# Two gates of a recurrent cell as four 64 by 64 products on the quarters of the TensorE array

## The chip, the core and the metric

The kernel runs on one NeuronCore of a Trainium2 chip. The metric is device time of one execution in microseconds. The granted TensorE clock was 0.999 of full speed in the profiled execution.

## The reference, cut to what matters

A stack of graph layers works on 3327 nodes with 64 features and a dense adjacency matrix `adj` (3327 by 3327). The first layer is two gated cells, one after the other, each with its own weights:

```python
def _ggc(x, adj, W, wih, whh, bih, bhh):
    m = adj @ (x @ W)
    gi = m @ wih.T + bih
    gh = x @ whh.T + bhh
    i_r, i_z, i_n = jnp.split(gi, 3, axis=-1)
    h_r, h_z, h_n = jnp.split(gh, 3, axis=-1)
    r = jax.nn.sigmoid(i_r + h_r)
    z = jax.nn.sigmoid(i_z + h_z)
    n = jnp.tanh(i_n + r * h_n)
    return (1.0 - z) * n + z * x
```

Three more layers follow: a ranked neighbour sum whose weights come from the order of the nonzeros in a row of `adj`, three products with the element-wise square of `adj`, and two plain hops with tanh. A layer norm with ReLU stands before each layer.

The change concerns the line of `n` in the second cell. There `h_n` and `i_n` must be kept apart, since `r` multiplies only the one; for `r` and `z` the two parts are simply added.

## The kernel before

**Layout.** The nodes are padded to 26 blocks of 128 and form two halves of 13 blocks. The halves are stacked on the 128 partitions, 64 features each. The destination nodes are cut into chunks of blocks (`CH`): chunks 0, 1 and 2 are 384 columns wide, chunk 3 is 512. Chunks 0 and 1 form one group, 2 and 3 the other. For each of the eight products with the matrix (numbered k = 0 to 7) and each chunk, L607 adds up two products per source block, one for each half, into the two partition halves of a PSUM bank. Only one group's matrix tiles are loaded at a time (`slots`, 20 buffers), and two consecutive products share the tiles where they can (`joint`).

**Order.** Each engine's order is written out by the program itself: `run` walks a list of units, and `propagate` issues a unit's matmuls. What follows a finished sum is a Python generator (`after_1` for the second cell), which is advanced between units as its counted-down time runs out (`spend`). So the instructions of a cell lie between the matmuls of the next sums, and between the mask builds of L466 on VectorE, which make 0/1 masks for the ranked product k = 2.

**Banks.** There are eight PSUM banks, four named `sum` and four named `temp`. `take` hands out the one that was given back longest ago; `give` returns it. The products of the gates, the mask products with `tri` (L307, followed by L521 on VectorE or L523 on ScalarE) and the transposes all draw on them.

**The cell.** `gru` first moves the finished sum into `both[c]` (L824 on ScalarE for one half of the nodes, L825 on VectorE for the other). `both[c][:, s]` has 128 rows for half `s`: the neighbour sum `m` in rows `upper(s)` and the state `x` in rows `upper(1 - s)`. `cells[:, cell, s, g, :]` holds the matching 128 by 64 weights of gate `g`: 0 and 1 are `r` and `z`, with weights in all 128 rows. Gate 2 is `h_n` and has weights in rows `upper(1 - s)` only, and gate 3 is `i_n`, in rows `upper(s)` only; the other rows are zero.

`gate(g)` (L873 to L877) takes one bank and issues two products of 128 rows by 64 columns, one per half of the nodes. The gates 0 and 1 go through a sigmoid on ScalarE (L881). Then L886 computes `(h_n + bias) * r` and L888 adds `i_n`, both on VectorE over all 128 partitions. L897 is the tanh on ScalarE, and L901 to L903 mix with `z` and the old state. In the first cell `h_n` was computed earlier by `ahead_of_cell`, so only the second cell runs gate 2 here. After the cell, `after_1` transposes the result back (L307), adds it to `xs` (L854) and runs the layer norm (L834 to L849) ahead of k = 2.

A matmul of f32 operands appears as two records in the profile, each with its weight load. All matmuls of this kernel are listed with 128 rows and 64 columns (128*64).

Of the kernel before, what the change touches and what calls it, by code (L numbers as in the profile page):

```python
# [13 lines left out]
ALU = mybir.AluOpType  # L14
# [77 lines left out]
def upper(n):  # L92
    return slice(n * D, (n + 1) * D)
# [3 lines left out]
def kernel(  # L97
# [9 lines left out]
    nc = tc.nc  # L107
# [16 lines left out]
    cells = const.tile([P, 2, 2, 4, D], F32, name="cells")  # L124
# [3 lines left out]
    both = [const.tile([P, 2, (b1 - b0) * P], F32, name=f"both{c}") for c, (b0, b1) in enumerate(CH[:NC])]  # L128
    both += [both[1][:, :, (CH[c][0] - CH[1][0]) * P:(CH[c][1] - CH[1][0]) * P] for c in PARTS]
    bcol = const.tile([P, NBIAS], F32, name="bcol")  # L130
# [57 lines left out]
    ahead = {}  # L188
# [110 lines left out]
    def width(c):  # L299
        return blocks(c) * P  # L300
# [15 lines left out]
    def take(sums=False, either=True):  # L316


        either = either and not sums
        pool = idle_sums if sums else idle_temps  # L320
        if either and idle_sums and (not pool or released[idle_sums[0]] < released[pool[0]]):
            pool = idle_sums
        for c in list(tasks):
            if not pool and c not in running:
                advance(c)
        i = pool.popleft()
        return i, banks[i]

    def give(i):
        released[i] = max(released) + 1  # L330
        (idle_sums if i < 4 else idle_temps).append(i)
# [21 lines left out]
    def advance(c):  # L353
        running.add(c)
        try:
            tasks[c][1] = next(tasks[c][0])
        except StopIteration:
            del tasks[c]
        running.discard(c)
# [463 lines left out]
    def evacuate_stacked(acc, c):  # L823
        nc.scalar.copy(both[c][upper(0), 0], acc[0][1][upper(0), :width(c)])  # L824
        nc.vector.tensor_copy(both[c][upper(1), 1], acc[1][1][upper(1), :width(c)])  # L825
        for i in {acc[0][0], acc[1][0]}:
            give(i)
# [37 lines left out]
    def gru(acc, c, bi, bh, cell, pace=1.0):  # L865

        w = width(c)
        evacuate_stacked(acc, c)
        yield 0.8 * pace
        at = dead.popleft()  # L870
        r, z, d = (slots[at].rearrange("p s w -> p (s w)")[:, i * CWM:i * CWM + w] for i in range(3))

        def gate(g):  # L873
            i, ps = take()
            for s in range(2):
                nc.tensor.matmul(ps[upper(1 - s), :w], cells[:, cell, s, g, :], both[c][:, s], start=True, stop=True)  # L876
            return i, ps  # L877

        for g, v in enumerate((r, z)):
            i, ps = gate(g)  # L880
            nc.scalar.activation(v, ps[:, :w], AF.Sigmoid, bias=bsum[:, cell, g:g + 1])  # L881
            give(i)
        nh = None if cell == 0 else gate(2)
        ni = gate(3)
        yield 1.0 * pace
        nc.vector.scalar_tensor_tensor(r, ahead[c] if nh is None else nh[1][:, :w], bcol[:, bh + 2:bh + 3], r,  # L886
                                       op0=ALU.add, op1=ALU.mult)
        nc.vector.tensor_tensor(r, r, ni[1][:, :w], ALU.add)  # L888
        give(ni[0])
        if nh is not None:  # L890
            give(nh[0])
        else:
            del ahead[c]
            if not any(ch in ahead for ch in GROUPS[c // 2]):
                rooms[c // 2].free()
        yield 1.0 * pace
        nc.scalar.activation(r, r, AF.Tanh, bias=bcol[:, bi + 2:bi + 3])  # L897
        yield 0.8 * pace
        for s in range(2):
            u = upper(1 - s)  # L900
            nc.vector.tensor_tensor(d[u], both[c][u, s], r[u], ALU.subtract)  # L901
        nc.vector.tensor_tensor(d, d, z, ALU.mult)
        nc.vector.tensor_tensor(d, d, r, ALU.add)  # L903
        if cell == 0:
            nc.vector.tensor_scalar(both[c][upper(0), 1], d[upper(0)], 0.0, None, op0=ALU.max)
        yield 2.4 * pace
        if cell == 0:
            nc.scalar.activation(both[c][upper(1), 0], d[upper(1)], AF.Relu)
            yield 1.0 * pace
        return at, d  # L910
# [27 lines left out]
    def after_0(c, acc):  # L938
        at, _ = yield from gru(acc, c, BI1, BH1, 0)
        dead.append(at)  # L940
        i, v = stacked_to_nodes(c, lambda s: ident[:, upper(1 - s)])
        yield 0.8
        yk = nodes(c)
        nc.vector.tensor_copy(flat(yk), v)
        give(i)
        y[1][c] = yk

    def after_1(c, acc):
        pace = 1.0 if c in GROUPS[0] else 1.2
        at, h2T = yield from gru(acc, c, BI2, BH2, 1, pace)  # L950
        v = transpose_to_nodes(h2T, c)
        dead.append(at)
        yield 0.8 * pace
        residual(v, c, relu=True)
        yk = nodes(c)
        yield from layernorm_relu(yk, c, TWO27, 1.2 * pace, squares_on_scalar=c in GROUPS[1])
        y[2][c] = yield from in_three(yk, c)
        yield 80.0 if c in GROUPS[1] else 14.0
        add_row(c, 3)
# [126 lines left out]
```

## Time and profile before

| | |
|---|---|
| time, median of 3 runs | 708.03 us (707.58 to 708.05) |
| the profiled execution's own time | 707.41 us |
| its span | 705.5 us |
| TensorE matmul busy | 680.6 us (96%), 5100 records |
| VectorE busy | 351.7 us (50%), 747 records |
| ScalarE busy | 271.3 us (38%), 421 records |
| GpSimd busy | 75.7 us (11%), 114 records |
| DMA | 201.31 MB, mean 285 GB/s |

The span runs from the first to the last instruction; the profiled execution's time is 1.9 us longer. Busy shares are means over stages that differ: the matrix streams through with little VectorE work in most of the span, while from some 180 to 330 us mask builds, ranked products and squares fill VectorE and ScalarE. The second cell runs at 163 to 231 us. Below, PE is TensorE, DVE is VectorE, ACT is ScalarE, POOL is GpSimd and SP is SyncE. In the chain of waits, a line has the start, the length and the engine, tile and line of one link; "issue" is time in which no wait is visible. In the timeline, a line has the start, the length, the engine, the line, the operation, out<-in, the shapes and the count, and in brackets the idle time before it with what ended it. In the table of stretches, the numbers are busy microseconds and instruction counts of each engine.

### The profile page before, as it was taken

What the parts mean: (1) busy time and instruction counts of PE and PEld (TensorE: products, weight loads), DVE (VectorE), ACT (ScalarE), POOL (GpSimd) and SP (SyncE); (2) the same over time, 40 slices, a digit from 0 to 9 for tenths busy, and PEclk for the clock granted to TensorE, in tenths of its full rate; (3) what the DMA queues carried; (4) which work ended last, traced back from release to release, by engine and by line L of the source; (5) the groups of instructions that cost most, each with busy time, mean ns of one, the idle gap of its engine ahead of it and who ended that gap; (6) DMA issues with size and microseconds to landing.
All of it is one profiled execution on the core that took longest, in us unless ns stands there. A gap on an engine that the chain in (4) does not pass through costs nothing.

```text
span 705.5 us, 12624 instructions
## 1 busy us (share of the span) xinstructions
PE 680.6 (96%) x5100; PEld 362.5 (51%) x5100; DVE 351.7 (50%) x747; ACT 271.3 (38%) x421; POOL 75.7 (11%) x114
## 2 busy tenths in 40 slices
PE   1999999999999999999999999999999999999997
PEld 1454666643545787677444444333344444344464
DVE  7566835633997889847533105425271565005101
ACT  1014100212136888888997206832166500000101
POOL 4300000002291233111100000000000000000000
PEclk9999999999999999999999999999999999999999
DMA  9999996089688952683799649963997399917991
GB/s 337 401 387 404 405 406 239 1 337 384 204 284 299 313 176 83 241 296 103 266 369 354 242 163 408 405 262 112 392 366 271 105 397 405 407 64 282 403 402 36
DMA packets 68549, 201.31 MB, mean 285 GB/s; under 512 B 7228, under 2 KB 8228, under 8 KB 68492
## 3 DMA queue, kind: packets, MB, share of 16 engines
q1 hardware_dynamic: 65596, 199.46, 76.1%
q8 instruction: 40, 0.66, 0.4%
q10 hardware_dynamic: 720, 0.85, 0.3%
q0 software_dynamic: 2176, 0.20, 0.2%
q14 instruction: 17, 0.14, 0.1%
HBM read 199.45 MB, written 0.85 MB: 284 GB/s over the span
## 4 chain that ended last, share of the span: by engine, by line
PE 84%; DVE 9%; ACT 4%; issue 1%; DMA 1%; SPq 0%; ACTq 0%; DVEq 0%
PE sum L607 70%; PE temp L307 5%; ACT adj L440 4%; DVE adj L466 3%; PE temp L542 2%; PE temp L876 2%; PE sum L307 1%; PE temp L774 1%; PE sum L876 1%; DVE e L521 1%; DMA bd<-in_weights 1%; DVE both L825 1%; DVE adj L901 1%; DVE st L842 0%; DVE t L836 0%
## 5 line engine op out<-in xcount | busy, mean ns | idle before, releaser
L607 PE MATMUL sum<-adj,y 128*64 128x384 f32 (+3 forms) x3016 | 533.6, 501 | 0.8 <-DVE y L849 0.6
L607 PEld LDWEIGHTS sum<-adj,y 128*64 128x64 f32 x3016 | 233.7, 137 | 246.3 <-issue 220.9
L440 ACT ACTIVATE adj<-adj 128x768 f32<-128x768 f32 (+1 forms) x175 | 143.6, 892 | 47.3 <-PE sum L607 24.6
L466 DVE TENSOR_SCALAR adj<-adj 128x768 bf16<-128x768 f32 (+3 forms) x208 | 114.7, 599 | 39.1 <-PE temp L542 31.1
L824 ACT COPY both<-sum 64x384 f32<-64x384 f32 (+3 forms) x17 | 8.1, 478 | 196.4 <-PE sum L607 196.3
L607 PE MATMUL sum<-e,both 128*64 128x384 bf16 (+1 forms) x624 | 78.4, 339 | 0.5 <-DVE e L521 0.4
L523 ACT ACTIVATE e<-temp,bitsb 128x384 int16<-128x384 f32 (+1 forms) x117 | 66.1, 606 | 15.0 <-PE temp L307 9.9
L825 DVE COPY both<-sum 64x384 f32<-64x384 f32 (+3 forms) x17 | 9.7, 568 | 113.6 <-ACT both L824 112.4
L442 DVE TENSOR_TENSOR adj<-adj 128x768 f32<-128x768 f32 (+1 forms) x33 | 31.5, 1003 | 52.2 <-DMA adj<-in_adjT 33.4
L307 PE MATMUL temp<-adj,tri 128*64 128x384 bf16 (+1 forms) x332 | 56.8, 341 | 0.5 <-DVE e L521 0.2
L845 POOL TENSOR_TENSOR st<-st,mhalf 128x6 f32<-128x6 f32 (+1 forms) x16 | 24.5, 1529 | 288.9 <-DVE st L843 288.9
L607 PEld LDWEIGHTS <-both 128*64 128x64 bf16 x624 | 46.5, 110 | 15.5 <-issue 2.2
L307 PEld LDWEIGHTS <-tri 128*64 128x64 bf16 x416 | 33.4, 110 | 15.3 <-issue 7.4
L521 DVE TENSOR_SCALAR e<-temp 128x384 int16<-128x384 f32 (+1 forms) x49 | 30.1, 617 | 21.1 <-ACT e L523 10.5
L471 POOL DMA_DIRECT2D adj<-totals x52 | 32.7, 630 | 51.5 <-PE temp L307 42.9
L803 DVE STREAM_TRANSPOSE both<-y 32x96 f32<-32x96 f32 (+1 forms) x128 | 35.6, 278 | 2.9
L542 PE MATMUL temp<-adj,behind 128*64 128x384 bf16 x208 | 30.3, 339 | 0.9 <-DVE adj L466 0.7
L819 DVE STREAM_TRANSPOSE y<-t 32x96 f32<-32x96 f32 (+1 forms) x64 | 17.8, 278 | 25.2 <-ACT t L810 24.3
L542 PEld LDWEIGHTS <-behind 128*64 128x64 bf16 x208 | 17.0, 110 | 17.6 <-issue 15.9
L755 DVE COPY t<-sum 128x384 f32<-128x384 f32 x6 | 3.3, 554 | 35.4 <-PE sum L607 35.4
L876 PE MATMUL temp<-both,cells 128*64 128x384 f32 (+1 forms) x68 | 17.7, 521 | 0.2 <-DVE both L825 0.2
L523 ACT ACTIVATE e<-sum,bitsb 128x384 int16<-128x384 f32 (+1 forms) x28 | 16.6, 599 | 2.5 <-PE sum L307 2.0
(132 smaller groups left out, 307.5 us busy)
## 6 DMA issues: line engine op xcount, KB each, us to landing
adj<-in_adjT SPq DMA_DIRECT2D x130, 768.0 KB, 8.5
adj<-in_adjT SPq DMA_DIRECT2D x104, 896.0 KB, 12.5
xs<-in_x SPq DMA_DIRECT2D x1, 640.0 KB
adj<-totals POOLq DMA_DIRECT2D x26, 3.0 KB, 5.3
adj<-totals POOLq DMA_DIRECT2D x26, 3.5 KB, 3.6
out<-xs ACTq DMA_DIRECT2D x2, 192.0 KB
out<-xs ACTq DMA_DIRECT2D x1, 256.0 KB
stage<-in_weights SPq DMA_DIRECT2D x2, 112.0 KB, 13.4
```

The costliest lines, as they stand in the source:

```text
L307: nc.tensor.matmul(out[hs], lhsT[:, hs], rhs, start=start, stop=stop)
L440: nc.scalar.activation(sq, v, AF.Square)
L442: nc.vector.tensor_tensor(sq, v, v, ALU.mult)
L466: nc.vector.tensor_scalar(t.mask.view[:rows, half], t.view()[:rows, half], 0.0, None, op0=ALU.not_equal)
L471: nc.gpsimd.dma_start(out=t.mask.view[P - 1:P], in_=totals[t.g][t.q:t.q + D + 1:D, :])
L521: nc.vector.tensor_scalar(wide[:, s], ps[:, :w], BITS, 0.0, op0=ALU.add, op1=ALU.max)
L523: nc.scalar.activation(wide[:, s], ps[:, :w], AF.Relu, bias=bitsb)
L542: nc.tensor.matmul(counts[c][1][s * D:(s + 1) * D, :w], behind[:, NQ - 1 - t.q:NQ - 1 - t.q + D], t.mask.view[:, s, t.cols(c)], start=firs ...
L607: nc.tensor.matmul(acc[h][1][h * D:(h + 1) * D, :w], yq[h], rhs[h], start=first and n == 0, stop=last and n == len(terms) - 1)
L803: nc.vector.transpose(to[at:at + 32, :, q], h[q * 32:(q + 1) * 32, :, s, f * 32:(f + 1) * 32])
L845: nc.gpsimd.tensor_tensor(st[:, 3, :n], st[:, 2, :n], mhalf[:, :n], ALU.pow)
L876: nc.tensor.matmul(ps[upper(1 - s), :w], cells[:, cell, s, g, :], both[c][:, s], start=True, stop=True)
```

## The change

In the second cell, gates 2 and 3 no longer go through `gate`. Two banks are taken, one for each half of the array's rows. Each product uses only the 64 rows that have weights: for half `s` of the nodes, gate 2 from rows `upper(1 - s)` into the bank of that row half, and gate 3 from rows `upper(s)` into the bank of the other. The results lie in partitions `upper(1 - s)` of either bank. So the four products occupy the four 64 by 64 quarters of the array, in the order (64, 64), (0, 64), (0, 0), (64, 0) of row and column. As `h_n` then lies in different banks for the two halves, L886 and L888 become two instructions each, on 64 partitions. The first cell is left as it is.

```diff
-        nh = None if cell == 0 else gate(2)
-        ni = gate(3)
-        yield 1.0 * pace
-        nc.vector.scalar_tensor_tensor(r, ahead[c] if nh is None else nh[1][:, :w], bcol[:, bh + 2:bh + 3], r,
-                                       op0=ALU.add, op1=ALU.mult)
-        nc.vector.tensor_tensor(r, r, ni[1][:, :w], ALU.add)
-        give(ni[0])
-        if nh is not None:
-            give(nh[0])
+        if cell == 1:
+
+            n = [take() for _ in range(2)]
+            for s in range(2):
+                u = upper(1 - s)
+                for row, g in ((1 - s, 2), (s, 3)):
+                    nc.tensor.matmul(n[row][1][u, :w], cells[upper(row), cell, s, g, :], both[c][upper(row), s],
+                                     start=True, stop=True)
+            yield 1.0 * pace
+            for s in range(2):
+                u = upper(1 - s)
+                nc.vector.scalar_tensor_tensor(r[u], n[1 - s][1][u, :w], bcol[u, bh + 2:bh + 3], r[u],
+                                               op0=ALU.add, op1=ALU.mult)
+            for s in range(2):
+                u = upper(1 - s)
+                nc.vector.tensor_tensor(r[u], r[u], n[s][1][u, :w], ALU.add)
+            for i, _ in n:
+                give(i)
         else:
+            ni = gate(3)
+            yield 1.0 * pace
+            nc.vector.scalar_tensor_tensor(r, ahead[c], bcol[:, bh + 2:bh + 3], r, op0=ALU.add, op1=ALU.mult)
+            nc.vector.tensor_tensor(r, r, ni[1][:, :w], ALU.add)
+            give(ni[0])
             del ahead[c]
```

## The prediction

> **What bounds the kernel now.** First the page's shares: TensorE (PE) is busy 96% of the span, VectorE (DVE) 50%. That average hides what matters here, so I went on to the places where the changed lines stand. L886 runs eight times, four of them in the second cell (at 165.6, 175.7, 216.3 and 225.9 us); I call these chunks 2, 3, 0 and 1, in order of time. Then busy time in stretches of 5 us:
>
> ```profile
> core 0: us, PE busy (x) PEld busy (x) DVE busy (x) ACT busy (x) POOL busy (x), PEclk, DMA share, GB/s
> 160.00:165.00 5.00, 5.00 (x30) 2.10 (x28) 0.56 (x1) 1.14 (x3) 0.00 (x0) 1.00 1.03 403
> ...
> 190.00:195.00 5.00, 5.00 (x34) 2.23 (x32) 4.93 (x12) 1.14 (x2) 1.26 (x2) 1.00 0.87 243
> 195.00:200.00 5.00, 5.00 (x34) 2.22 (x32) 4.96 (x12) 0.51 (x1) 4.56 (x6) 1.00 0.86 277
> 200.00:205.00 5.00, 5.00 (x39) 2.30 (x36) 5.00 (x10) 3.20 (x6) 4.11 (x7) 1.00 1.01 380
> 205.00:210.00 5.00, 5.00 (x48) 3.30 (x48) 5.00 (x9) 2.85 (x6) 4.80 (x9) 1.00 0.76 251
> ```
>
> At chunk 2 DVE is nearly idle and PE alone is full; from 180 to 213 us DVE is full as well. Which of the two ends last is told by the chain of waits:
>
> ```profile
> 212.80 0.54 DVE adj L466
> 213.37 0.57 DVE both L825
> 213.94 0.04 issue
> 213.99 1.18 PE temp L876 x5
> ...
> 225.42 0.56 DVE e L521
> 225.98 0.54 DVE adj L886
> 226.54 0.56 DVE adj L888
> 227.10 0.04 issue
> 227.14 0.35 PE sum L307 x2
> ```
>
> Chunk 0's gates start when DVE, behind a row of mask builds (L466), gets to L825. And chunk 1's own L886 and L888 are links of the chain. From 154 to 178 us, and from 214 to 225 us, the chain is PE but for short hand-overs.
>
> The timeline of PE gives the price of a gate (four records, two passes for each of two products):
>
> ```profile
> 163.40 1.46 PE L876 MATMUL sum<-both,cells 128*64 128x384 f32 x8
> 164.69 1.46 PE L876 MATMUL temp<-both,cells 128*64 128x384 f32 x8
> 165.98 0.60 PE L607 MATMUL sum<-adj,y 128*64 128x512 f32 x2
> ...
> 174.14 1.43 PE L876 MATMUL sum<-both,cells 128*64 128x512 f32 x4
> 175.00 1.43 PE L876 MATMUL temp<-both,cells 128*64 128x512 f32 x4
> ```
>
> Start to start, two gates of 384 columns take 1.29 us: 0.645 each, a record 0.32 with the two column halves side by side. At 512 columns a gate takes 0.86.
>
> **What the Trainium skill says.** *TensorEngine Tiling (Array Packing)*, Key Properties: tiles execute independently, but changing the tiling mode, "not just tile", drains TensorE. No matmul of the kernel before is anything but 128*64, so its trace shows no such change. *TensorE: Matmul & The Clock Gate*, Part 3, has row and column tiles running together (four row tiles measured 3.07 times faster). The trace agrees for column halves: at 215.98 an L607 product already runs in one half while the last record of the gate starts in the other at 216.30. Row tiles it doesn't show. *TensorEngine Tiling*, Gotcha 1: row tiles need different PSUM banks; the change uses two banks, one per row half, as many as before.
>
> **The change, part by part.** The order of instructions on each engine stays as it was, apart from the changed lines; banks get other numbers. SP's and POOL's queues, and so all DMAs, are untouched.
>
> *PE, taken away.* Gates 2 and 3 of a chunk were four products on all 128 rows, two slots of two. If the four quarters run together, the pair takes the time of one gate: −0.645 us for chunks 2, 0 and 1, −0.86 for chunk 3, 2.8 in all.
>
> *PE, added.* Two mode changes per chunk, each costing d. From below 0. From above: the tail of a record (486 ns recorded against 323 from start to start, so 163) plus a weight load with no cover (137): 0.30. I take 0.2: the tail, plus the 51 ns by which a record after a stall is longer (537 against 486). Recorded ends are modelled, so this is an estimate.
>
> *DVE, added.* L886 and L888 each become two instructions on 64 partitions. Half the partitions is not half the time: L901 on 64 partitions takes 556 ns, L902 on 128 takes 559. So one L886 (616 ns at 384 columns, 751 at 512) and one L888 (555, 687) are added per chunk: about 1.2 us, 1.45 for chunk 3. Semaphore gaps are under 0.05.
>
> *A wait that moves.* Before, L886 waited for gate 2 alone and gate 3 ran behind it. Now the first DVE instruction waits for all four quarters. At 384 columns without drain they end when gate 2 did; d comes on top. At 512 columns the last passes would start at 175.41 and end at 176.0 (592 ns each) against 175.6: +0.4.
>
> Now what lies on the path.
>
> *Chunk 2.* DVE was idle for 2.1 us before L825 at 172.0; 1.2 us more on the cell's way (tanh, L901 to L903, done at 169.9) still fits. PE is the chain: −0.645 + 2d, carried to chunk 3.
>
> *Chunk 3.* This is where the cover is thin:
>
> ```profile
> 175.68 0.75 DVE L886 SCALAR_TENSOR_TENSOR adj<-sum,bcol,adj 128x512 f32<-128x512 f32 x1 [1.42 <-PE sum L876]
> 176.54 0.69 DVE L888 TENSOR_TENSOR adj<-adj,temp 128x512 f32<-128x512 f32 x1
> 177.14 1.49 DVE L466 TENSOR_SCALAR adj<-adj 127x768 bf16<-127x768 f32 x3
> 179.12 0.56 DVE L854 SCALAR_TENSOR_TENSOR xs<-temp,xs 128x384 f32<-128x384 f32 x1 [0.49 <-PE temp L307]
> ```
>
> DVE starts 0.41 + d later and has 1.41 more to do, 1.82 + d at L466. The only slack up to 213 us is the idle time before L854: without PE's wait it would start 0.57 earlier (L466 comes every 0.469). So L854 moves by 1.25 + d, and with it everything on DVE: L903 (PE's transposes at 184.4 already wait for it) and L825 at 213.4. PE, now ahead, waits at both. With what chunk 2 gave: 1.25 + d − 0.645 + 2d = 0.6 + 3d.
>
> *Chunk 0.* PE is the chain from 214.0: −0.645 + 2d. The added DVE work falls into 2.1 us without work before 220.1. A mask product that takes one of the freed banks at about 218.2 now waits for the third DVE instruction instead of L888; its margin was 0.7, so this costs 0 to 0.3, and I take 0.1.
>
> *Chunk 1.* PE before it: −0.645 + 2d. Then the chain passes through L886 and L888: +1.2, of which 0.25 is recovered, as DVE no longer idles before the L521 at 227.5. After it DVE is full to 240 us (4.8 of 5 in 230 to 240), and PE idles 1.06 us in 235 to 240 waiting for it, so +0.95 stays.
>
> *Sum.* 0.6 + 3d − 0.65 + 2d + 0.1 − 0.65 + 2d + 0.95 = about 0.35 + 7d; with d = 0.2, **+1.7 us**. After 284 us PE and ScalarE work in lockstep, then PE alone from 365 to the end; I let the delay go through. Against the profiled execution (705.5 us span, 707.41 in all) that is 709.1; that execution lay 0.6 under the median of 708.03. Forecast for the median: 709.7 us. A measurement of this kernel can tell about 0.2%, 1.4 us, from no change.
>
> **The rivals.**
> 1. *Mode changes are free* (d = 0): +0.35, 708.4 us, not slower. One mechanism with one price: at d = 0.15 the sum passes 1.4 us, and below it the change can't be told from none. For it: weight loads are pulled ahead all over the trace. Against it: the skill's sentence on the drain.
> 2. *Only two quarters at a time* (row halves don't overlap for f32 passes): no PE time saved, and DVE starts a slot pair later in chunk 3. Chunk 2 +0.4, chunk 3 1.25 + 0.86 + 0.2, chunk 0 +0.5, chunk 1 +1.35: +4.5, 712.5 us. Against it: the page's measured row tiles; for it: nothing in this trace shows them.
> 3. *The DVE delay is absorbed* and PE's saving stays. One L466 at 207.6 took 1957 ns instead of 550, so DVE has a stall of 1.4 us that could fall elsewhere; ScalarE, which is the chain from 336 to 365 us, could swallow the rest. With d near 0.1: 2.8 − 0.8 saved, 706.0 us.
>
> **How the numbers follow.** Forecast 0.58, of which 0.45 over and 0.13 under the bound (d between 0 and 0.3 spans 0.35 to 2.45); rival 1 0.20 (0.18 within, 0.02 faster); rival 2 0.12, all slower; rival 3 0.10 (0.07 faster, 0.03 within). Faster 0.09, same 0.34, slower 0.57. The range of 707.4 to 712.4 leaves out rival 3 and half of rival 2; the forecast's own is 708.4 to 710.5.
>
> **What would show it.** Right: the quarters of a chunk starting within some 0.02 us of each other, two passes of 0.32 us; a gap of about 0.2 us before the first and after the last; the L854 that stood at 179.1 about a microsecond later, PE waiting at the transposes of 184.4, and L825 later by as much as L854; about 5 us more DVE time in all. Wrong: L854 later while L825 at 213.4 is not (absorbed), quarters starting in pairs (rival 2), or L607 following the quarters without a gap (rival 1). The whole argument fails if DVE has gaps between 180 and 213 us after the change.

## The result, and the profile after

The changed kernel took **709.93 us** (median of 9 runs, 709.46 to 710.34) against 708.03 for the kernel before in the same series: a ratio of 1.0027, 95% interval 1.0019 to 1.0035. That is 1.9 us slower; 1.7 were forecast, and the time lies in the range. The size agrees better than the steps do: three terms were mis-sized, in both directions.

The page of the kernel after, first part:

```profile
span 708.4 us, 12629 instructions
...
PE 680.2 (96%) x5100; PEld 350.5 (49%) x5100; DVE 356.6 (50%) x755; ACT 271.5 (38%) x421; POOL 76.7 (11%) x114
```

The same number of matmul records, eight DVE instructions more, and 4.9 us more DVE time (356.6 less 351.7; some 5 were forecast). PE's busy time hardly falls (680.2 against 680.6 us), although the gates got shorter. Shares don't tell what happened; the places do.

The quarters themselves, in PE's timeline of the kernel after, at chunk 2 and at chunk 3:

```profile
164.58 1.46 PE L876 MATMUL sum<-both,cells 128*64 128x384 f32 x8
165.97 0.88 PE L889 MATMUL temp<-both,cells 64*64 64x384 f32 x8
166.78 1.51 PE L607 MATMUL sum<-adj,y 128*64 128x512 f32 x6
...
175.44 0.64 PE L889 MATMUL temp<-both,cells 64*64 64x512 f32 x1
175.45 0.65 PE L889 MATMUL sum<-both,cells 64*64 64x512 f32 x2
175.46 1.05 PE L889 MATMUL temp<-both,cells 64*64 64x512 f32 x2
175.93 0.59 PE L889 MATMUL sum<-both,cells 64*64 64x512 f32 x2
175.94 0.59 PE L889 MATMUL temp<-both,cells 64*64 64x512 f32 x1
```

Four products start within 0.02 us, run two passes, and the next product follows. At chunk 2 the eight records of gates 0 and 1 and the eight quarter records take 166.78 − 164.58 = 2.20 us, where the four gates took 2.58 (163.40 to 165.98 before). A pair of gates at full rows took 1.29; four quarters side by side would be 0.645. So two mode changes cost 2.20 − 1.29 − 0.645 = 0.265 us up to the start of L607, and 0.05 more in L607's first record (643 ns, the later ones 592): 0.31 in all, or **0.15 to 0.16 us each** (0.2 was taken). PE gains 0.645 − 0.31 = 0.33 per chunk of 384 columns.

DVE's timeline behind them, at chunk 3, and further down at chunk 1:

```profile
176.67 0.76 DVE L894 SCALAR_TENSOR_TENSOR adj<-temp,bcol,adj 64x512 f32<-64x512 f32 x1 [1.58 <-PE temp L889]
177.46 0.74 DVE L894 SCALAR_TENSOR_TENSOR adj<-sum,bcol,adj 64x512 f32<-64x512 f32 x1
178.23 0.69 DVE L898 TENSOR_TENSOR adj<-adj,sum 64x512 f32<-64x512 f32 x1
178.96 0.68 DVE L898 TENSOR_TENSOR adj<-adj,temp 64x512 f32<-64x512 f32 x1
179.56 1.48 DVE L466 TENSOR_SCALAR adj<-adj 127x768 bf16<-127x768 f32 x3
180.97 0.54 DVE L854 SCALAR_TENSOR_TENSOR xs<-temp,xs 128x384 f32<-128x384 f32 x1
...
227.14 0.62 DVE L894 SCALAR_TENSOR_TENSOR adj<-sum,bcol,adj 64x384 f32<-64x384 f32 x1
227.79 0.61 DVE L894 SCALAR_TENSOR_TENSOR adj<-temp,bcol,adj 64x384 f32<-64x384 f32 x1
228.43 0.56 DVE L898 TENSOR_TENSOR adj<-adj,temp 64x384 f32<-64x384 f32 x1
229.02 0.55 DVE L898 TENSOR_TENSOR adj<-adj,sum 64x384 f32<-64x384 f32 x1
...
229.69 0.54 DVE L521 TENSOR_SCALAR e<-temp 128x384 int16<-128x384 f32 x1
```

Half the partitions, the same duration: 0.76 against 0.75 on 128, and 0.69 against 0.69. The idle 0.49 us before L854 has gone; it is the cover that the prediction named. At chunk 1 L521 follows without its idle 0.25 us. The table of stretches:

```profile
core 0: us, PE busy (x) PEld busy (x) DVE busy (x) ACT busy (x) POOL busy (x), PEclk, DMA share, GB/s
185.00:190.00 5.00, 3.73 (x50) 2.28 (x52) 4.93 (x11) 0.00 (x0) 1.61 (x2) 1.00 0.57 198
...
205.00:210.00 5.00, 5.00 (x45) 3.39 (x43) 5.00 (x11) 4.46 (x9) 4.80 (x8) 1.00 0.79 252
```

DVE has hardly a gap (34.56 of 35 us busy from 180 to 215), and PE, which is ahead, waits for it. In PE's timeline:

```profile
186.27 1.15 PE L307 MATMUL sum<-ident,adj 128*64 128x64 f32 x32 [1.80 <-DVE adj L917]
...
213.78 1.51 PE L607 MATMUL sum<-adj,y 128*64 128x384 f32 x8 [0.86 <-DMA adj<-in_adjT]
```

The first line is the wait at the transposes (0.21 us in the kernel before). The second is a wait for a matrix tile just ahead of chunk 0 (0.21 us in the kernel before, too); it costs nothing here, since DVE reaches L825 only at 215.20, right behind a row of L466. The margin is nil: the L824 that follows this wait ends at 215.17.

**Where the time came from.** The table follows one ScalarE instruction at each place through the kernels, as the difference of its start from the kernel before. Each row is one execution. The executions differ already at 35 us into the span, ahead of any changed instruction (after is 1.18 later there, the other kernels 0.40 to 1.46), so that offset is taken off. The heads give the place in the kernel before; the experiments are those of the next section.

| shift in us at | 171.4, chunk 3's L824 | 181.1, past its L854 | 214.9, chunk 0's gate | 217.7, behind chunk 0's gates | 223.8, behind chunk 1's gates | 227.1, its tanh | 232.7 | 271.8 | 287.4 | end |
|---|---|---|---|---|---|---|---|---|---|---|
| after | −0.38 | +0.66 | +0.65 | +0.31 | −0.12 | +1.36 | +1.04 | +1.00 | +1.73 | +1.74 |
| e1_bank_swap | 0 | 0 | −0.01 | −0.01 | −0.01 | 0 | −0.27 | −0.33 | +0.40 | +0.41 |
| e2_after_swap | −0.38 | +0.66 | +0.65 | +0.31 | −0.12 | +1.36 | +1.33 | +1.35 | +1.35 | +1.51 |
| e3_dve_split | −0.05 | +0.80 | +0.79 | +0.79 | +0.73 | +2.20 | +2.17 | +2.19 | +2.19 | +2.20 |
| e4_gate_banks | −0.33 | −0.73 | −0.69 | −1.03 | −1.39 | −1.39 | −1.40 | −1.40 | −1.37 | −1.38 |
| e5_apart | +0.61 | +1.20 | +1.19 | +1.78 | +2.34 | +2.34 | +2.34 | +2.51 | +3.55 | +3.55 |
| e6_only_23 | −0.39 | +0.65 | +0.28 | +0.28 | +0.28 | +0.28 | +0.28 | +0.28 | +0.31 | +0.31 |
| e8_gate_banks_zero | −0.33 | −0.72 | −0.96 | −1.30 | −1.67 | −1.67 | −1.67 | −1.65 | −1.65 | −1.64 |
| e9_zero_act_look | 0 | 0 | −0.22 | −0.22 | −0.22 | −0.22 | −0.22 | −0.21 | −0.18 | −0.17 |

In the row of after, PE's saving shows three times (−0.38 at chunk 2, −0.34 at chunk 0, −0.43 before chunk 1's L894), DVE's added work twice (+1.04 at chunk 3, +1.48 at chunk 1). Some 0.05 of the first and the third saving is not PE's: e3, whose matmuls are those of the kernel before, shows −0.05 and −0.06 at the same steps, and PE's own products behind chunk 2 start 0.33 earlier. The last step, +0.73 between 271.8 and 287.4, lies 40 us behind the last changed instruction and was not forecast. In PE's timeline of the kernel after it is two waits:

```profile
271.71 0.41 PE L307 MATMUL sum<-adj,tri 128*64 128x512 bf16 x2
272.28 0.68 PE L607 MATMUL sum<-e,both 128*64 128x384 bf16 x6 [0.17 <-ACT e L523]
...
288.54 1.08 PE L607 MATMUL sum<-adj,y 128*64 128x512 f32 x4 [0.19 <-DVE e L521]
```

The first of them stands, in the kernel before, 0.21 us behind the mask product ahead of it:

```profile
269.53 0.41 PE L307 MATMUL temp<-adj,tri 128*64 128x512 bf16 x2
269.74 0.68 PE L607 MATMUL sum<-e,both 128*64 128x384 bf16 x6
```

In the kernel after it is 0.57 (272.28 behind 271.71). The product at 288.54 takes in `adj` and `y`, and nothing that L521 makes, so what it waits for is a bank that L521 still reads; for the other it may be the bank or the mask `e`. The chain of waits of the kernel after begins at that product of 288.54: the profile follows it back no further. The engines' orders are the same as before at these places, but the banks have other numbers since the cell, because the changed code gives the two banks back in another order. That was a suspicion, and the first experiments were made for it.

### The profile page after: what moved, and what is told of

Same layout as the page of the kernel before. It is cut to its first block, busy times and chain, and to the rows that moved or that the text cites. A ratio compares the mean times of both kernels' runs of the same rounds, so it can differ in the third digit from the quotient of the medians.

```text
span 708.4 us, 12629 instructions
## 1 busy us (share of the span) xinstructions
PE 680.2 (96%) x5100; PEld 350.5 (49%) x5100; DVE 356.6 (50%) x755; ACT 271.5 (38%) x421; POOL 76.7 (11%) x114
## 4 chain that ended last, share of the span: by engine, by line
PE 55%; DMA 1%; DVE 1%; ACT 0%; issue 0%; POOL 0%; ACTq 0%; DVEq 0%; SPq 0%; POOLq 0%
PE sum L607 52%; PE temp L307 3%; PE temp L774 1%; DMA adj<-in_adjT 1%; DMA out<-xs 1%; DVE both L825 0%; ACT both L824 0%; POOL st L845 0%; DVE xs L1033 0%; ACT t L1030 0%; DVE e L521 0%; PE sum L307 0%; ACT t L753 0%; DVE t L836 0%; DVE y L849 0%
## 5 line engine op out<-in xcount | busy, mean ns | idle before, releaser
L607 PE MATMUL sum<-adj,y 128*64 128x384 f32 (+3 forms) x3016 | 531.8, 502 | 1.6 <-DMA adj<-in_adjT 0.9
L607 PEld LDWEIGHTS sum<-adj,y 128*64 128x64 f32 x3016 | 228.6, 137 | 252.4 <-issue 226.7
L466 DVE TENSOR_SCALAR adj<-adj 128x768 bf16<-128x768 f32 (+3 forms) x208 | 114.7, 599 | 40.3 <-PE temp L542 32.3
L824 ACT COPY both<-sum 64x384 f32<-64x384 f32 (+3 forms) x17 | 8.1, 477 | 195.3 <-PE sum L607 189.6
L607 PE MATMUL sum<-e,both 128*64 128x384 bf16 (+1 forms) x624 | 73.0, 339 | 0.7 <-DVE e L521 0.4
L523 ACT ACTIVATE e<-temp,bitsb 128x384 int16<-128x384 f32 (+1 forms) x120 | 67.5, 608 | 13.6 <-PE temp L307 8.1
L825 DVE COPY both<-sum 64x384 f32<-64x384 f32 (+3 forms) x17 | 9.7, 569 | 110.1 <-ACT both L824 108.9
L307 PE MATMUL temp<-adj,tri 128*64 128x384 bf16 (+1 forms) x334 | 49.3, 342 | 2.3 <-DVE e L521 1.2
L607 PEld LDWEIGHTS <-both 128*64 128x64 bf16 x624 | 40.5, 110 | 19.5 <-issue 7.0
L521 DVE TENSOR_SCALAR e<-temp 128x384 int16<-128x384 f32 (+1 forms) x47 | 28.9, 618 | 20.9 <-ACT e L523 10.3
L307 PEld LDWEIGHTS <-tri 128*64 128x64 bf16 x416 | 27.6, 110 | 18.9 <-issue 11.6
L564 POOL MEMSET adj<- 128x768 f32 (+1 forms) x2 | 1.6, 802 | 145.5 <-PE sum L607 145.5
L791 PE MATMUL temp<-ident,y 128*64 128x128 f32 x24 | 2.4, 351 | 14.9 <-DVE y L849 14.9
```

Of the source, the lines that this page charges most:

```text
L307: nc.tensor.matmul(out[hs], lhsT[:, hs], rhs, start=start, stop=stop)
L466: nc.vector.tensor_scalar(t.mask.view[:rows, half], t.view()[:rows, half], 0.0, None, op0=ALU.not_equal)
L521: nc.vector.tensor_scalar(wide[:, s], ps[:, :w], BITS, 0.0, op0=ALU.add, op1=ALU.max)
L523: nc.scalar.activation(wide[:, s], ps[:, :w], AF.Relu, bias=bitsb)
L607: nc.tensor.matmul(acc[h][1][h * D:(h + 1) * D, :w], yq[h], rhs[h], start=first and n == 0, stop=last and n == len(terms) - 1)
```

## The experiments

Each kernel ran on the same chip as the kernel before; ratios are to it.

**e1_bank_swap: the kernel before with the two banks given back in the other order.**

```diff
-        give(ni[0])
         if nh is not None:
             give(nh[0])
-        else:
+        give(ni[0])
+        if nh is None:
             del ahead[c]
```

> The kernel before with nothing but the order in which the two banks of gates 2 and 3 are given back turned round (gate 2's first), so that later banks are handed out as in the changed kernel. Theory 1 (bank numbers cause the late part of the loss): no shift up to 265 us, then PE waits for a bank that was not waited for before, +0.35 us near 270 us and +0.4 near 287, about +0.7 in all. Rival (the delay itself upsets the later stage): nothing moves, 0.0.

708.45 us, ratio 1.0006 (0.9999 to 1.0013). The trace shows both halves of what the bank order does. Nothing moves until 229 us, then 0.33 are gained, and between 271.8 and 287.4 it loses 0.73, as much as the kernel after does there. So the late waits do come from the order of the banks alone. The net is +0.4, not the +0.7 of the waits.

**e2_after_swap: the kernel after with its banks given back in the other order.**

```diff
-            for i, _ in n:
+            for i, _ in reversed(n):
                 give(i)
```

> The changed kernel with its two banks given back in the opposite order. Theory 1: the two late waits near 272 and 290 us go, so about 0.7 us less than the changed kernel: +1.1 us against before instead of +1.9. Rival: as the changed kernel, +1.9.

709.27 us, ratio 1.0017 (1.0007 to 1.0026); this interval overlaps that of after, so the two are told apart by the traces and not by the times. The row equals that of after up to 227.1; then the gain of 0.32 behind chunk 1 is missing, and so is the late step. At 271.94 the product is back to 0.22 us behind its mask product. Of the 1.74 us of after, 0.23 net is bank order, not the 0.7 expected, since the gain goes with the waits; about 1.5 us is the change proper.

**e3_dve_split: the gates of the kernel before, DVE's work in halves.**

```diff
-        nc.vector.scalar_tensor_tensor(r, ahead[c] if nh is None else nh[1][:, :w], bcol[:, bh + 2:bh + 3], r,
-                                       op0=ALU.add, op1=ALU.mult)
-        nc.vector.tensor_tensor(r, r, ni[1][:, :w], ALU.add)
+        for u in ((slice(0, P),) if nh is None else (upper(1), upper(0))):
+            nc.vector.scalar_tensor_tensor(r[u], ahead[c] if nh is None else nh[1][u, :w], bcol[u, bh + 2:bh + 3], r[u],
+                                           op0=ALU.add, op1=ALU.mult)
+        for u in ((slice(0, P),) if nh is None else (upper(1), upper(0))):
+            nc.vector.tensor_tensor(r[u], r[u], ni[1][u, :w], ALU.add)
```

> The matmuls of the kernel before (gates on all 128 rows) with only the VectorE side of the change: L886 and L888 as two instructions each on 64 partitions, banks given back as before. Theory 1 (the added VectorE time is the cost, hidden for chunks 2 and 0, exposed for 3 and 1): at L854 of 179 us +0.9 (1.45 of added work less 0.57 of slack), L825 of 213 us +0.9, after chunk 1 another +0.95, in all +1.85 us. Rival (the mode changes of the array are the cost, VectorE's additions are hidden): 0.0 to +0.3.

710.19 us, ratio 1.0033 (1.0021 to 1.0045). At chunk 3 +0.85, near the forecast; at chunk 1 +1.47 and nothing of it recovered, where 0.95 was expected. DVE's timeline at chunk 1:

```profile
227.36 1.26 DVE L887 SCALAR_TENSOR_TENSOR adj<-temp,bcol,adj 64x384 f32<-64x384 f32 x2
228.66 1.14 DVE L890 TENSOR_TENSOR adj<-adj,sum 64x384 f32<-64x384 f32 x2
229.72 0.21 DVE L232 COPY brow<-temp 128x64 f32<-128x64 f32 x1
...
230.24 0.56 DVE L521 TENSOR_SCALAR e<-sum 128x384 int16<-128x384 f32 x1 [0.25 <-PE sum L307]
```

PE's timeline of the same kernel:

```profile
229.85 0.35 PE L307 MATMUL sum<-adj,tri 128*64 128x384 bf16 x2 [1.61 <-DVE adj L890]
```

Two corrections follow. The four halves last from 227.36 to the copy of L232 at 229.72, 2.36 us, where the two whole ones took 1.11 (225.90 to 227.01): 1.25 more. Another 0.11 lies ahead of them: the first half starts 0.59 behind the L521 of 226.77, the whole one 0.48 behind that of 225.42. And the idle 0.25 us before L521 does not vanish: the mask product that L521 reads waits for the bank that the last half (L890) holds, so it moves along. In the kernel after the product got the bank that the third half gives free (it starts at 229.05, when L898 on `temp` has ended), which is the other order of giving back.

**e4_gate_banks: the quarters, with one bank for each gate, so that DVE's work stays whole.**

```diff
-        nh = None if cell == 0 else gate(2)
-        ni = gate(3)
+        nh = None
+        if cell == 0:
+            ni = gate(3)
+        else:
+            nh, ni = take(), take()
+            for s in range(2):
+                for (i, ps), g, row in ((nh, 2, 1 - s), (ni, 3, s)):
+                    nc.tensor.matmul(ps[upper(1 - s), :w], cells[upper(row), cell, s, g, :], both[c][upper(row), s],
+                                     start=True, stop=True)
```

> The four quarter products of the change, but the banks by gate instead of by row half: gate 2 of both halves into one bank, gate 3 into the other, so that L886 and L888 stay single instructions on 128 partitions as before. Theory 1 (quarters run together and save 0.36 us per chunk net of two mode changes; VectorE's split was the loss): faster than before by 0.9 to 1.2 us, 706.9 to 707.1. Rival (row halves that write one bank are kept apart in time, or the mode changes eat the saving): 0.0 or up to +1 us.

**706.6 us, ratio 0.9986 (0.9978 to 0.9993)**: faster than both kernels. PE's timeline of it at chunk 3, with the second passes left out, and DVE's:

```profile
174.87 0.64 PE L890 MATMUL sum<-both,cells 64*64 64x512 f32 x1
174.87 0.64 PE L890 MATMUL temp<-both,cells 64*64 64x512 f32 x1
174.88 0.64 PE L890 MATMUL sum<-both,cells 64*64 64x512 f32 x1
174.89 0.64 PE L890 MATMUL temp<-both,cells 64*64 64x512 f32 x1
```

```profile
176.07 0.75 DVE L893 SCALAR_TENSOR_TENSOR adj<-sum,bcol,adj 128x512 f32<-128x512 f32 x1 [1.60 <-PE temp L890]
176.93 0.69 DVE L895 TENSOR_TENSOR adj<-adj,temp 128x512 f32<-128x512 f32 x1
177.54 1.49 DVE L466 TENSOR_SCALAR adj<-adj 127x768 bf16<-127x768 f32 x3
```

Two products from different row halves write one bank, each into its own half of the partitions, and still start within 0.02 us. The Trainium skill, *TensorEngine Tiling (Array Packing)*, Gotcha 1, says that row tiles cannot access the same bank at once; here, with different partitions of the bank, they did, with the same length of 0.64 us as in the kernel after, and the measurement decides. So the split of DVE's work was no price of the quarters: it came from giving each row half its own bank. With it gone, every chunk keeps a saving: −0.33, −0.40, −0.34 and −0.36 between the places of the table.

e3 and e4 are the two parts of the change. Their ends sum to +2.20 − 1.38 = +0.82, and both together (e2) give +1.51. Of the 0.69 between them, 0.59 is seen at chunk 3: apart, +0.85 and −0.40; together +1.04, since there DVE sets the time and PE's saving is worth nothing.

**e5_apart: gate 2's quarters put between gates 0 and 1, gate 3's behind them: four mode changes per chunk instead of two.** DVE's work is whole, as in e4.

```diff
+        def half_gate(g):
+            i, ps = take()
+            for s in range(2):
+                row = 1 - s if g == 2 else s
+                nc.tensor.matmul(ps[upper(1 - s), :w], cells[upper(row), cell, s, g, :], both[c][upper(row), s],
+                                 start=True, stop=True)
+            return i, ps
+
+        nh = None
...
-        nh = None if cell == 0 else gate(2)
-        ni = gate(3)
+            if cell == 1 and g == 0:
+                nh = half_gate(2)
+        ni = gate(3) if cell == 0 else half_gate(3)
```

> Banks by gate as in the run before, but the quarter products set apart: gate 2's two products on 64 rows between the gates r and z, gate 3's after z. So there are four mode changes per chunk instead of two, and only two quarters at a time. Theory 1 (a mode change costs 0.14 us by itself, whoever runs beside whom): the four gates take as long as before plus 4 x 0.14 = 0.56 us; in the trace L824 of chunk 3 (171.4 us) comes 0.56 later than before; the whole about +1.5 to +2.5 us, as PE is the chain at chunks 2, 0 and 1. Rival (the gaps belong to filling and emptying four quarters at once): L824 later by 0.0 to 0.1, whole 0.0.

711.28 us, ratio 1.0048 (1.0033 to 1.0064). PE's timeline at chunk 2:

```profile
164.87 0.82 PE L876 MATMUL sum<-both,cells 128*64 128x384 f32 x4
165.62 0.86 PE L883 MATMUL sum<-both,cells 64*64 64x384 f32 x4
166.41 0.87 PE L876 MATMUL temp<-both,cells 128*64 128x384 f32 x4
167.20 0.86 PE L883 MATMUL temp<-both,cells 64*64 64x384 f32 x4
168.00 1.08 PE L607 MATMUL sum<-adj,y 128*64 128x512 f32 x4
```

The next product starts 168.00 − 164.87 = 3.13 us after the first gate, against 2.58 before, or 0.55 more, and 0.05 lies again in L607's first record; the shift of chunk 3's L824 is +0.61. That is four changes at **0.15 us**. Two quarters alone take as long as a full gate, so here nothing is saved. Each of the four chunks adds 0.56 to 0.61, chunk 3 too, so that +2.34 stands behind the cell, within the +1.5 to +2.5 expected. The whole is worse, by waits behind it: +0.17 up to 271.8 and +1.04 between 271.8 and 287.4, where the same two products wait as in after. This kernel, too, takes its banks in another order; that this is the cause here was not tried.

**e6_only_23: the change in chunks 2 and 3 alone.**

```diff
-        if cell == 1:
+        if cell == 1 and c in GROUPS[1]:
...
```

The lines left out give the other chunks gates 2 and 3 as in the kernel before; the edit is shown against the kernel after.

> The change made in the chunks 2 and 3 alone; chunks 0 and 1 keep the two gates on 128 rows with whole VectorE instructions. Theory 1 (VectorE is full from 179 to 213 us, and what chunk 3 adds goes through to the end): L839 near 181 us and L881 near 215 us both +0.65, and still about +0.65 at the end (give or take 0.3 for other bank numbers); whole +0.7 us. Rival (the delay of chunk 3 is taken up again, and the loss comes from chunks 0 and 1): back to 0.0 by 240 us.

708.27 us, ratio 1.0009 (1.0000 to 1.0019). The +0.65 of chunk 3 arrives at 181.1 as in after, but 0.37 of it is gone at 214.9. DVE's timeline there, and POOL's:

```profile
206.75 6.18 DVE L466 TENSOR_SCALAR adj<-adj 127x768 bf16<-127x768 f32 x13
214.05 0.56 DVE L825 COPY both<-sum 64x384 f32<-64x384 f32 x1 [1.12 <-ACT both L824]
214.64 2.08 DVE L466 TENSOR_SCALAR adj<-adj 127x768 bf16<-127x768 f32 x3
```

```profile
207.13 7.39 POOL L947 DMA_DIRECT2D lasty<-both  x4 [0.73 <-DVE both L940]
214.50 0.86 POOL L564 MEMSET adj<- 128x896 f32 x1
```

The same thirteen L466 took 7.63 us in the kernel before, one of them 1.96. In this run POOL cleared its tile (L564) at 214.5, behind L825, and not at 208.3, and the long L466 went along with it: the one at 214.64 took 1.15 us. So rival 3 has a mechanism: DVE's delay is swallowed if POOL's clearing falls late enough. In the kernels after, e2 and e3 it fell ahead of L825, as in before. POOL's trace shows why it fell late: the four DMA issues ahead of it took 7.39 us, where the kernel before has

```profile
206.09 2.23 POOL L928 DMA_DIRECT2D lasty<-both  x4 [0.20 <-issue]
```

The first of the four took 5.90 us instead of 0.74 and ended at 213.03, just behind the row of thirteen L466, which ended at 212.93. So in e6 DVE's row held POOL up; in the kernel before, POOL's clearing held DVE up.

**e7_zero_act and e8_gate_banks_zero: POOL's clearing given to ScalarE**, in the kernel before and in e4.

```diff
-        nc.gpsimd.memset(v, 0.0)
+        nc.scalar.activation(v, mhalf[:, 0:1].to_broadcast([P, w]), AF.Copy, scale=0.0)
```

> The kernel before, with the clearing of a tile near 208 us (last_sources, on POOL, 0.86 us) done by ScalarE instead; the gates stay as they were. The point is the DVE instruction on L466 that lies beside POOL's clearing and takes 1.96 us instead of 0.55. Theory (the clearing on POOL holds that instruction up): it takes about 0.55 us, L825 behind it starts up to 0.6 us earlier (then bound by ScalarE's L824), and the whole is 0.4 to 0.6 us faster, about 707.3 against 707.8. Rival (it is long for another reason, or DVE is not what L825 waits for): still about 1.95 us, or no gain, 707.8.

> The quarters with one PSUM bank for each gate (as in e4_gate_banks), with the clearing near 208 us on ScalarE as in e7_zero_act. Theory (in e4 L825 waited for ScalarE's L824 anyway, which ended 0.03 us before it): equal to e4 within 0.2 us, about 706.5. Rival (the delay of DVE there still counts, so both gains add): 706.1 or less.

e7: 708.21 us, ratio 1.0002 (0.9995 to 1.0010), no gain where 0.4 to 0.6 us were expected. e8: 706.72 us, ratio 0.9981 (0.9974 to 0.9987), equal to e4 within the intervals; its trace ends 0.26 us earlier by the shift (−1.64 against −1.38), so a small gain may be in it. Where e7's gain went is read from one more run of the same kernel.

**e9_zero_act_look: e7's kernel, for its trace.**

> The same kernel as e7_zero_act, for its trace. The question is where the 1.4 us went that the DVE instruction on L466 no longer takes. Theory 1 (used up before L825): ScalarE's clearing of 0.94 us puts its reads of banks (L523 at 204) and with them PE back by 0.85 us, as in e8_gate_banks_zero, so that L824 ends 0.5 us or more later than in the kernel before, DVE waits about 1.2 us for it and L825 starts within 0.2 us of where it stood. Theory 2 (given back later): L825 starts 0.4 to 0.6 us earlier, and a wait after 215 us takes it back.

708.52 us in this one execution. Theory 1 holds, but for L824, which moved by a little less than the 0.5 us expected. DVE's timeline, and ScalarE's:

```profile
207.08 6.27 DVE L466 TENSOR_SCALAR adj<-adj 127x768 bf16<-127x768 f32 x13
214.51 0.56 DVE L825 COPY both<-sum 64x384 f32<-64x384 f32 x1 [1.17 <-ACT both L824]
```

```profile
205.24 0.94 ACT L564 ACTIVATE adj<-mhalf 128x896 f32<-128x896 f32 x1
206.09 1.51 ACT L523 ACTIVATE e<-temp,bitsb 128x384 int16<-128x384 f32 x3
```

The thirteen L466 are 1.36 us shorter, as expected. But ScalarE's L523 starts 0.86 later by the shift, PE with it, and L824 0.41 later; L825 now waits 1.17 us for L824 and moves by only −0.22. DVE was one of two that end together here; with the clearing on ScalarE, the stall of 1.4 us was worth 0.2. What it would be worth without ScalarE's 0.94 us of clearing was not tried.

## Why the prediction came true, and which of its steps did not

- **What bounds where: right.** Chunk 2 and PE before chunk 1 shortened, chunk 3 and chunk 1 grew by DVE's work, DVE was full up to chunk 0 and L825 moved as far as L854 (+0.65 and +0.67).
- **A mode change: right in kind, smaller.** 0.15 to 0.16 us in after and 0.15 in e5, against 0.2 taken. Of the two parts of the 0.2, the longer record (51 ns) is there, and the tail (163 ns taken) is 0.10 to 0.11 us of added distance. The Trainium skill, *TensorEngine Tiling (Array Packing)*, Key Properties, has the drain without a price; the trace agrees that a change costs time, and this is its size here. Rival 1 (free) and rival 2 (two quarters at a time) are both out.
- **Chunk 3: mis-sized.** "L854 moves by 1.25 + d", so 0.6 + 3d, 1.2 us with chunk 2's gain; measured +0.66. DVE's extra 1.43 us (1.41 forecast) and the absorbed 0.57 held. The term that failed is the wait for all four quarters: 0.41 + d = 0.61 forecast. In chunk 3 of the kernel before, the two products of a gate run one pass (0.43 us) apart, and the forecast left that stagger in the quarters. They start together, so the first DVE instruction stood 0.19 earlier by the shift, or 0.19 later than chunk 2's −0.38 alone would put it: of the term, about d is left. Error: −0.42 us.
- **PE's savings: too small, as d was taken too large.** −0.38, −0.34 and −0.43 against −0.245 each with d at 0.2; the 0.1 for a mask product at chunk 0 did not show. Together −0.5 us.
- **Chunk 1's DVE work: about right, with the wrong reason for a part.** +1.48 at the tanh and +1.16 past it, against 1.2 and 0.95. The halves cost more than the durations say (below), and e3 and e2 show that the idle time before L521 goes only if the bank order lets it.
- **"I let the delay go through": wrong by +0.7.** It ignored that the order of the banks changed for all that follows. e1 shows that order alone costs 0.73 us between 271.8 and 287.4 and gains 0.33 ahead of it; e2 shows the waits gone with the other order. The forecast had priced bank numbers at one place, with 0.1.
- **Sum.** Against the forecast: −0.42 (the wait), −0.13, −0.20 and −0.19 (PE), +0.21 (chunk 1's DVE) and +0.70 (banks), together about 0. The total agrees with 1.7 since errors of up to 0.7 us cancel, which is luck, and a reader should trust the steps and not the total.
- **Rival 3 (absorbed): not in this kernel, but real.** e6 shows 0.37 us absorbed where POOL's clearing lies behind L825. The clearing falls late where POOL's DMA issues ahead of it are held until the row of L466 ends (7.39 us in e6, 2.23 in before, after and e2 to e5). Why they are held there was not settled: in before as in e6 the first of them starts 0.38 us into the row. The stall of L466 is shown to go with the clearing by e6, e8 and e9.

## What to carry to other kernels

Before you split a unit's work over tiles of the array, look who reads the results: the layout of the output banks decided here between +1.9 (0.2 of it the order of giving back) and −1.1 us, for the same four products. Give to one bank what one instruction will read. Price a change of buffer order over the whole rest of the kernel, by searching for products that wait on a reader of their bank, and try both orders, for it is one line.

## What the runs showed of the hardware that was not expected

- A change between 128 by 64 and 64 by 64 products costs PE 0.15 to 0.16 us, both ways, at f32: some 0.10 of distance ahead of the first record and 0.05 in it.
- Four quarters of f32 run side by side (starts within 0.02 us), and start together at chunk 3 too, where the two column halves of the kernel before are one pass apart.
- Row halves that write different partition halves of one bank run side by side (e4).
- The DVE halves follow each other without overlap: 228.43 to 229.02 is 0.59 for an instruction of 0.56, while L466, 0.55 long, comes every 0.469. Dependent instructions on 128 partitions do the same in e3 (the `z` mix, 232.53 and 233.12, 0.56 long). That they lie on 64 partitions is not enough to cause it: the L466 of 179.56 starts 0.08 us before the last half (178.96, 0.68 long) ends. The halves begin at partition 64 and at partition 0 in turn, and L466 begins at 0 like the half ahead of it. Whether this change of the first partition causes it, or an order kept through their common tile, was not tried.
- A POOL memset holds up a DVE instruction: L466 took 1.96 us beside it, and the group of thirteen 7.63 us, against 6.17 in e8, where every one took 546 to 550 ns. In before and in e6 (1.15 us) the record of the long L466 ends 0.42 us behind that of the memset. The Trainium skill, *SBUF — State Buffer*, section Who interferes with whom, has `tensor_scalar` among those that can contend with GpSimd, one side then blocking fully. The trace agrees with the blocking; in which mode L466 runs is not in it.
